# A fourth resident row group in a fused deformable-convolution kernel, with the second image's input kept between its passes and its table built backwards

## Chip, cores and metric

The kernel runs on one NeuronCore of a Trainium2 chip. The metric is the device time of one execution in microseconds (us). The kernel before took 3757.64 us, the median of three runs (3755.66 to 3757.74).

## What is computed

Input `x` is (2, 256, 128, 128) in fp32: two images, 256 channels, 128 by 128 pixels. Two layers follow each other, both of the form x + conv(group norm(x)). Cut to what matters:

```python
# layer 0: deformable 3x3 convolution on the normalised input
g = gn(x)                                    # 32 groups of 8 channels
offset = conv2d(g, w_off, b_off)             # 18 channels: dy, dx for each of 9 taps
mask = sigmoid(conv2d(g, w_mask, b_mask))    # 9 channels
# each tap of each pixel samples g at a fractional place: four corners, bilinear weights
sampled = bilinear(g, base + offset) * mask
x = x + einsum('bckhw,ock->bohw', sampled, w_conv) + b_conv
# layer 1: eight low-rank experts (a 1x3 into 8 channels, a 3x1 back to 256), mixed by probs
x = x + einsum('e,ebchw->bchw', probs, experts(gn(x)))
```

Group norm needs the mean and variance of a whole image before its first pixel can be normalised. So layer 0 needs statistics of `x`, and layer 1 statistics of layer 0's whole result.

## The kernel before, in words

**The table.** Sampling is done by gathers from a table in device memory, one per image. Each of its cells (a padded pixel) holds the 256 normalised channels of that pixel and those of the pixel below it: 512 floats, 2 KB. Two neighbouring cells, 4 KB, are the four corners of one sample. `frame` (L133) writes the zero cells around a table. To make the rest, `x` is normalised, TensorE transposes it from channels on partitions to pixels on partitions, ScalarE or VectorE copies the result out of PSUM into a tile of rows, and `store_cells` (L195) writes each row twice, as upper and as lower half of a cell.

**Sizes.** A group is 8 image rows (`GR`), a chunk 4 (`CR`): 16 groups (`NG`) or 32 chunks (`NCH`) an image. A tile of a group of `x` holds 1 MB (8 KB a partition), of a chunk half of that.

**The head** (L418 to L502) loads all of image 0, takes its statistics (L437), writes both frames (L453) and makes table 0. Of the loaded groups the first `XB + XR` = 6 stay on chip for the residual.

**The stream** (L814 to L842) is one loop over 2304 units, 1152 an image. A unit is one tap of one image row: 128 samples. In step s of it, `gather` (L546) issues the indirect DMA of unit s + 15 from GpSimd's queue (128 x 4 KB = 512 KB each, 15 tiles in turn), `product` (L556, ScalarE) multiplies the first corner of unit s + 3, `add` (L563, VectorE) adds the other three corners with three operations, `turn` (L570) transposes the sample on TensorE, `keep` (L580, ScalarE) copies it from PSUM, and `apply_tap` (L586, TensorE) multiplies with the convolution's weights. After the nine taps of a chunk `residual` (L596) adds `x` in place, `result_stats` (L602) takes the statistics for layer 1, and `store_x1` (L606) writes a finished group to the scratch tensor `x1`, unless `stays` (L283) says that the group remains on chip.

**Work between the units.** Everything else is a piece that `put` (L522) hangs on a slot, the number of the unit at whose step it is issued. The order of instructions on each engine, and of DMAs on SP's queue (SyncE's), is the order in which this loop meets them. Engines run in order, and so does SP: a DMA that must wait for a tile holds back the ones behind it. Pieces that matter here:
- `load_x` (L527) loads group g + 1 of the image at 54 slots before group g begins (L789), for the offsets (`offsets_of`, L298) and the residual.
- `table_beside(1)` (L610) makes image 1's table during image 0's units. From slot 4, every 8 slots, it loads a chunk into pool `tx` (three tiles) and takes its statistics (`of_stats`, L621, 14 and 18 slots later). After the norm's small pieces it loads all 32 chunks again from slot 324, one every 22 slots, normalises them in place (L631, 20 slots after the load), transposes and copies them (L635, L638) and writes their cells (L663, 33 slots after the load), going down the image. Row 0 of each tile of rows is copied from the tile before (L626).
- `second` (L803) runs layer 1 of image 0 during image 1's units, from the last chunk up, one chunk every 33 slots, with `cx`, `cxn` and `ch` pools of 4, 1 and 4 tiles (L804). Chunks whose group stayed on chip are used in place, the others are loaded from `x1` (L685).

**The tail** (L845 to L858) does layer 1 of image 1, by groups.

**Where groups of x live.** `x_tile` (L278) takes a tile of pool `xr` (`XR` = 3 tiles) for the last three groups of each image and for groups 3 to 5 of image 0, else one of pool `xp` (`XB` = 3 tiles) in turn. `stays` keeps the last three groups of image 0 and the last six of image 1.

Of the kernel before, what the change touches and what calls it, by code (L numbers as in the profile page):

```python
# [31 lines left out]
F32 = mybir.dt.float32  # L32
I32 = mybir.dt.int32
AF = mybir.ActivationFunctionType
# [4 lines left out]
P = 128  # L39
B, C, H, W = 2, 256, 128, 128  # L40
NH = C // P
# [6 lines left out]
CR = 4  # L48
NCH = H // CR
N = CR * W  # L50
GR = 8
CPG = GR // CR
NG = H // GR
GN = GR * W
WP = W + 3
HP = H + 3
CELL = 2 * C
# [4 lines left out]
UPG = UPC * CPG  # L62
UPI = UPG * NG
UNITS = B * UPI
GA = 15
# [1 line left out]
TL = 1  # L67
KL = 2
LM = 8
XB, XR = 3, 3  # L70


@with_exitstack
def layers(ctx, tc, x, w_om, b_om, w_cv, b_cv, w_in, w_out, probs, out):
    nc = tc.nc
# [5 lines left out]
    cp = ctx.enter_context(tc.tile_pool(name="const", bufs=1))  # L81
# [20 lines left out]
    )  # L102
    eps = cp.tile([P, 1], F32, name="eps")
    nc.vector.memset(eps, EPS)
    zero = cp.tile([P, CELL], F32, name="zero")
    nc.vector.memset(zero, 0.0)


# [14 lines left out]
    bias = cp.tile([P, NO], F32, name="bias")  # L123
# [9 lines left out]
    def frame(b):  # L133

        t = tables[b]
        side = t[WP - 1 : WP - 1 + (HP - 1) * WP].rearrange("(r c) e -> r c e", c=WP)[:, 0:3]
        z3 = zero.unsqueeze(1).broadcast_to([P, 3, CELL])
        nc.sync.dma_start(t[0:P], zero)
        nc.sync.dma_start(t[P : WP - 1], zero[0 : WP - 1 - P])
        nc.sync.dma_start(t[(HP - 1) * WP + 2 : (HP - 1) * WP + 2 + W], zero)  # L140
        nc.sync.dma_start(side[0:P], z3)
        nc.sync.dma_start(side[P : HP - 1], z3[0 : HP - 1 - P])
        nc.sync.dma_start(t[HP * WP - 1 : HP * WP + 2], zero[0:3])


    def norm_pieces(stats, small, psum, tag, name):
# [33 lines left out]
    def cells(b, y0, ny):  # L180
        rows = tables[b][(y0 + 2) * WP : (y0 + 2 + ny) * WP]
        return rows.rearrange("(r c) e -> c r e", c=WP)[2 : 2 + W]
# [5 lines left out]
    def transposes(ps, xt, rows):  # L188
        for i, r in enumerate(rows):
            for h in range(NH):  # L190
                nc.tensor.transpose(
                    ps[:, i, h * P : (h + 1) * P], xt[:, h, r * W : (r + 1) * W], ident
                )

    def store_cells(b, y, px, r, n):  # L195

        rows = px[:, r]
        pairs = bass.AP(rows.tensor, rows.offset, [rows.ap[0], [C, n], [1, CELL]])
        nc.sync.dma_start(cells(b, y + r, n), pairs)

    def store_last(b, row):

        nc.sync.dma_start(cells(b, H - 1, 1)[:, 0, 0:C], row)
        nc.sync.dma_start(cells(b, H - 1, 1)[:, 0, C:CELL], zero[:, :C])


    def offset_pieces(norm, oc, psum, tag, name):
# [62 lines left out]
    def pool(stack, name, bufs, **kw):  # L270
        return stack.enter_context(tc.tile_pool(name=name, bufs=bufs, reuse_waits="tile", **kw))

    xp = pool(ctx, "x", XB, side="right")
    xr = pool(ctx, "x_stay", XR, side="right")

    def x_tile(b, g):  # L278
        if g >= NG - XR or b == 0 and XB <= g < XB + XR:
            return xr.tile([P, NH, GN], F32, tag="xr", name=f"x_{b}_{g}")  # L280
        return xp.tile([P, NH, GN], F32, tag="xt", name=f"x_{b}_{g}")

    def stays(b, g):  # L283
        return g >= NG - XR - (XB if b == B - 1 else 0)
# [8 lines left out]
    xts = {}  # L293
# [124 lines left out]
    with ExitStack() as s:  # L418
# [6 lines left out]
        stats = hs.tile([P, NH, NCH, 6], F32, name="hstats")  # L425
        xv = view(x, 0)
        xs = []
        for g in range(NG):
            if g < XB + XR:
                xt = xts[0, g] = x_tile(0, g)  # L430
# [46 lines left out]
        head_norm(0)  # L477
        for g in range(NG):
            px = hp.tile([P, GR + 1, C], F32, tag="hp", name=f"hpx_{g}")
            nc.gpsimd.tensor_copy(px[:, 0], last[:, GR] if g else zero[:, :C])  # L480
            if g != 1 and g + 1 < NG:
                head_norm(g + 1)
            for i in range(0, GR, 2):
                ps = ht.tile([P, 2, C], F32, tag="t", name=f"hpt_{g}_{i}")
                transposes(ps, xs[g], (i, i + 1))
                if i % 4 == 0:
                    nc.scalar.copy(px[:, 1 + i : 3 + i], ps)
                else:
                    nc.vector.tensor_copy(px[:, 1 + i : 3 + i], ps)  # L489
                if g == 0:  # L490
                    store_cells(0, -1, px, i, 2)

                for piece in samples[: 2 if g < 2 else 1]:
                    piece()
                del samples[: 2 if g < 2 else 1]
            if g == 1:
                head_norm(2)
            if g > 0:
                store_cells(0, GR * g - 1, px, 0, GR)
            last = px  # L500
        store_last(0, last[:, GR])
        assert not samples  # L502


# [17 lines left out]
    def put(slot, piece, opens=False):  # L522
        sched[slot].append(piece)
        if opens:
            opened.add(slot)
# [82 lines left out]


    def table_beside(b):  # L610
        xq = pool(sides, "tx", 3)
        pq = pool(sides, "tpx", 2)
        held = {}
        xv = view(x, b)
        stats = st.tile([P, NH, NCH, 6], F32, tag="tstats", name=f"tstats_{b}")

        def load(j, what):
            held[what, j] = xq.tile([P, NH, N], F32, tag="tx", name=f"{what}_{b}_{j}")
            nc.sync.dma_start(held[what, j], xv[:, :, j * N : (j + 1) * N])

        def of_stats(j, h):  # L621
            nc.vector.bn_stats(stats[:, h, j], held["xs", j][:, h])

        def start(j):
            px = held["px", j] = pq.tile([P, CR + 1, C], F32, tag="tp", name=f"tpx_{b}_{j}")
            nc.vector.tensor_copy(px[:, 0], held["px", j - 1][:, CR] if j else zero[:, :C])  # L626

        def normalise(j, h):
            _, rstd, shift = norms0[b]
            v = held["xt", j][:, h]  # L630
            nc.scalar.activation(v, v, AF.Identity, bias=shift[:, h : h + 1], scale=rstd[:, h : h + 1])  # L631

        def turn_rows(j, i):
            ps = held["ps", j, i] = p_m.tile([P, 2, C], F32, tag="m", name=f"tpt_{b}_{j}_{i}")
            transposes(ps, held["xt", j], (i, i + 1))  # L635

        def keep_rows(j, i):
            nc.scalar.copy(held["px", j][:, 1 + i : 3 + i], held.pop(("ps", j, i)))  # L638

        slot = 4  # L640
        for j in range(NCH):
            put(slot, lambda j=j: load(j, "xs"))
            for h in range(NH):
                put(slot + 14 + 4 * h, lambda j=j, h=h: of_stats(j, h), True)
            slot += 8
        slot += 36
        norms0[b], pieces = norm_pieces(stats, st, p_m, "m", f"0_{b}")
        for piece in pieces:
            put(slot, piece)
            slot += 2  # L650
        offs[b], pieces = offset_pieces(norms0[b], oc, p_m, "m", str(b))
        for n, piece in enumerate(pieces):
            put(slot + 2 * n, piece)
        slot += 4
        for j in range(NCH):
            put(slot, lambda j=j: load(j, "xt"))
            for h in range(NH):
                put(slot + 20 + 3 * h, lambda j=j, h=h: normalise(j, h))
            put(slot + 24, lambda j=j: start(j))
            for n, i in enumerate(range(0, CR, 2)):  # L660
                put(slot + 26 + 4 * n, lambda j=j, i=i: turn_rows(j, i))
                put(slot + 28 + 4 * n, lambda j=j, i=i: keep_rows(j, i))
            put(slot + 33, lambda j=j: store_cells(b, CR * j - 1, held["px", j], 0, CR))  # L663
            slot += 22
        put(slot + 14, lambda: store_last(b, held["px", NCH - 1][:, CR]))
        return slot + 15


    def experts(b, norm, pools, psums, put_, rows, order, first, step, ahead, early=0):
# [107 lines left out]
    def expert_pools(stack, *bufs):  # L777
        return [pool(stack, name, n) for name, n in zip(("cx", "cxn", "ch"), bufs)]


    for b in range(B):
        stats1[b] = st.tile([P, NH, NCH, 6], F32, tag=f"stats{b}", name=f"stats1_{b}")
    for G in range(B * NG):
        b, g = divmod(G, NG)
        slot = UPG * G
        if g == 0:
            put(slot - 98, lambda b=b: load_x(b, 0))
        if g + 1 < NG:
            put(slot - 54, lambda b=b, g=g: load_x(b, g + 1))  # L789
        if (b, g) != (0, 0):  # L790
            for n, piece, opens in offsets_of(b, g):
                put(slot - 68 - GA + n, piece, opens)
    norms1 = [None] * B
    tabled = table_beside(1)
    assert tabled < UPI - UPG
    put(UPI - 16, sides.close)
    slot = UPI + LM + 10
    norms1[0], pieces = norm_pieces(stats1[0], st, p_m, "m", "1_0")
    for piece in pieces:
# [1 line left out]
        slot += 2  # L801

    def second(slot):  # L803
        pools = expert_pools(sides, 4, 1, 4)  # L804
        psums = ((p_m, "m"), (p_m, "m"))
        experts(0, norms1[0], pools, psums, put, CR, range(NCH - 1, -1, -1), slot + 36, 33, 33)

# [93 lines left out]
```

## Time and profile before

| what | value |
|---|---|
| median of three runs | 3757.64 us |
| profiled execution, its own time | 4080.06 us |
| its span (first to last instruction) | 4078.3 us |
| first gather issued | 155.7 us |
| last product of the stream | 3869.8 us |
| PE, PEld busy | 3493.9 us, 1854.9 us |
| VectorE (DVE), ScalarE (ACT), GpSimd (POOL) busy | 3355.3, 1841.9, 2290.3 us |
| bytes moved by DMA | 1444.29 MB, 354 GB/s over the span |
| of these by the gathers (queue q0) | 1208.11 MB |
| of these by SP's queue (q1) | 232.92 MB |

PE is TensorE's matmul, PEld its weight load. The page gives busy time by engine, a strip of 40 slices, the DMA queues, and groups of equal instructions with their mean time and with the idle time just before them, by what ended it. Times of single instructions come from one profiled execution, which is longer than the timed runs. VectorE's instructions overlap a little at their ends, so their mean time (481 ns for the adds of L566) is more than busy time by count (2963.7 us for 6912).

### The profile page before, as it was taken

The numbers are of one execution on the slowest core, as the hardware profiler recorded it, in microseconds if no ns is written. First come the engines' busy times: TensorE is split into PE (matmuls) and PEld (weight loads), VectorE is DVE, ScalarE is ACT, GpSimd is POOL, SyncE is SP. The second block draws the span as 40 slices with busy tenths as digits, with TensorE's granted clock in tenths as the row PEclk, the third lists the DMA queues.
The fourth block names the chain that finished last, engine by engine and source line by source line (L and its number), as shares of the span: only waits on it lengthen the run. The fifth ranks groups of instructions, "written<-read, shape, count | busy, mean of one in ns | idle before, by whom it ended". The sixth has DMA issues, their size and how long they took to land. (4 is left out here: it accounts for less than half of the span.)

```text
span 4078.3 us, 51366 instructions
## 1 busy us (share of the span) xinstructions
PE 3493.9 (86%) x13916; PEld 1854.9 (45%) x13916; DVE 3355.3 (82%) x7922; ACT 1841.9 (45%) x3883; POOL 2290.3 (56%) x2337
## 2 busy tenths in 40 slices
PE   3588888888888888988888999988999998888999
PEld 3444434444444444444444554444554555444433
DVE  6499988898888888988888888888898888888822
ACT  2344444455454554554444444444444444444421
POOL 0366655666666566666666665656666565656500
PEclk9699999999999999999999999999999999999999
DMA  9999999999999999999899999999999999999843
GB/s 366 368 377 379 380 356 354 375 385 388 375 402 396 374 404 394 387 398 367 325 336 349 359 371 347 365 365 348 364 361 370 356 361 356 351 335 344 304 150 124
DMA packets 427186, 1444.29 MB, mean 354 GB/s; under 512 B 42110, under 2 KB 43262, under 8 KB 426772
## 3 DMA queue, kind: packets, MB, share of 16 engines
q0 software_dynamic: 331776, 1208.11, 78.3%
q1 hardware_dynamic: 95124, 232.92, 15.1%
q8 instruction: 113, 1.85, 0.2%
q14 instruction: 173, 1.42, 0.1%
HBM read 1312.88 MB, written 127.97 MB: 353 GB/s over the span
## 5 line engine op out<-in xcount | busy, mean ns | idle before, releaser
L566 DVE SCALAR_TENSOR_TENSOR acc<-g,wt,acc 128x256 f32<-128x256 f32 x6912 | 2963.7, 481 | 417.0 <-ACT acc L560 250.3
L550 POOL DMA_INDIRECT g<-table,cidx x2304 | 2279.5, 989 | 1438.9 <-DVE acc L566 523.1
L591 PE MATMUL po<-sm,wcv 128*128 128x512 f32 x4608 | 2483.9, 621 | 278.8 <-issue 129.9
L584 ACT COPY sm<-ptr 128x512 f32<-128x512 f32 x1152 | 671.7, 583 | 1797.3 <-PE ptr L576 1035.4
L576 PEld LDWEIGHTS ptr<-idp,acc 128*128 128x128 f32 x4608 | 626.6, 145 | 1567.8 <-issue 1070.4
L560 ACT ACTIVATE acc<-g,wt 128x256 f32<-128x256 f32 x2304 | 1063.2, 506 | 81.5 <-DMA g<-table,cidx 59.0
L576 PE MATMUL ptr<-idp,acc 128*128 128x128 f32 x4608 | 929.2, 284 | 158.9 <-DVE acc L566 56.6
L591 PEld LDWEIGHTS po<-sm,wcv 128*128 128x128 f32 x4608 | 746.2, 197 | 343.8 <-issue 167.3
L319 PE MATMUL pu<-wus,x 128*128 128x81 f32 (+2 forms) x1600 | 297.2, 313 | 4.9 <-issue 3.3
L319 PEld LDWEIGHTS pu<-wus,x 128*128 128x128 f32 x1600 | 239.4, 200 | 8.0 <-issue 4.3
L707 PE MATMUL ph<-xcn,win 128*64 128x254 f32 (+3 forms) x1152 | 191.4, 474 | 16.0 <-issue 12.5
L600 DVE SCALAR_TENSOR_TENSOR x<-po,bcv,x 128x512 f32<-128x512 f32 x128 | 95.4, 745 | 64.5 <-remote 39.2
L745 DVE TENSOR_TENSOR xc<-pe,xc 128x512 f32<-128x512 f32 x92 | 60.3, 684 | 98.1 <-issue 79.1
L707 PEld LDWEIGHTS ph<-xcn,win 128*64 128x64 f32 x1152 | 84.1, 144 | 102.2 <-issue 76.2
L721 PE MATMUL pe<-h,wout 128*128 128x256 f32 (+1 forms) x384 | 126.4, 457 | 1.8 <-DVE xc L745 1.1
L714 ACT ACTIVATE h<-ph,pr 128x256 f32<-128x256 f32 (+1 forms) x48 | 26.2, 547 | 173.3 <-PE ph L707 139.1
L604 DVE BATCH_NORM_STATS2 stats<-x 128x6 f32<-128x512 f32 x128 | 87.7, 685 | 0.1
L721 PEld LDWEIGHTS pe<-h,wout 128*128 128x128 f32 x384 | 67.2, 191 | 41.1 <-issue 37.6
L745 DVE TENSOR_TENSOR x<-pe,x 128x512 f32<-128x512 f32 x36 | 23.1, 684 | 65.9 <-PE pe L736 62.3
L736 PE MATMUL pe<-h,wout 64*128 64x128 f32 (+1 forms) x752 | 69.9, 321 | 0.8 <-issue 0.8
L334 PE MATMUL om<-u,idp 128*128 128x216 f32 x192 | 53.1, 358 | 20.1 <-ACT u L328 11.7
L489 DVE COPY hpx<-hpt 128x512 f32<-128x512 f32 x32 | 21.1, 687 | 55.2 <-DMA table<-hpx 45.3
(92 smaller groups left out, 779.5 us busy)
## 6 DMA issues: line engine op xcount, KB each, us to landing
g<-table,cidx POOLq DMA_INDIRECT x2304
x<-in_x_dram SPq DMA_DIRECT2D x32, 1024.0 KB
table<-tpx SPq DMA_DIRECT2D x32, 1024.0 KB
table<-hpx SPq DMA_DIRECT2D x15, 2048.0 KB
x<-x SPq DMA_DIRECT2D x23, 1024.0 KB
out_dram<-xc SPq DMA_DIRECT2D x46, 512.0 KB
xs<-in_x_dram SPq DMA_DIRECT2D x32, 512.0 KB
xt<-in_x_dram SPq DMA_DIRECT2D x32, 512.0 KB
```

The lines of the kernel that those rows point to most:

```text
L319: nc.tensor.matmul(held["ps", j][:, lo:hi], lhsT=xt[:, h, r * W : (r + 1) * W], rhs=w[:, lo - i + 2 : hi - i + 2], start=(i == 2 and h == ...
L550: nc.gpsimd.indirect_dma_start(out=gt[:], out_offset=None, in_=tables[b][:, :], in_offset=bass.IndirectOffsetOnAxis(ap=idx[:, rr, k : k + ...
L560: nc.scalar.activation(acc, gts[u][:, 0:C], AF.Copy, scale=wt[:, 0, rr, k : k + 1])
L566: nc.vector.scalar_tensor_tensor(accs[u], gt[:, q * C : (q + 1) * C], wt[:, q, rr, k : k + 1], accs[u], ALU.mult, ALU.add)
L576: nc.tensor.transpose(pts[u // 2][:, h, (r % 2) * W : (r % 2 + 1) * W], acc[:, h * P : (h + 1) * P], ident)
L584: nc.scalar.copy(sms[u // CR][:, :, (r - 1) * W : (r + 1) * W], pts.pop(u // 2))
L591: nc.tensor.matmul(pos_[b, ci, m], lhsT=wcv[:, h, k, m * P : (m + 1) * P], rhs=sms[u // CR][:, h], start=(k == 0 and h == 0), stop=(k == K ...
L600: nc.vector.scalar_tensor_tensor(v, pos_.pop((b, ci, m)), bcv[:, m : m + 1], v, ALU.add, ALU.add)
L604: nc.vector.bn_stats(stats1[b][:, m, ci], xts[b, ci // CPG][:, m, at_ : at_ + N])
L707: nc.tensor.matmul(o[:, :, to], lhsT=win[:, h, tap], rhs=pairs[:, t, :, of], start=(q == 0), stop=(q == 5),)
L721: nc.tensor.matmul(ps[t][:, m], lhsT=wout[:, 2 * t, m * P : (m + 1) * P], rhs=hs[ci], start=(banks or m == 0), stop=False,)
L745: nc.vector.tensor_tensor(v, ps[t][:, ms].rearrange("p h (j x) -> p h j x", x=W), v, ALU.add)
```

## The change

`XR` goes from 3 to 4, and the tiles for it are found by making others fewer: `zero` is half as wide, pool `tx` has two tiles instead of three, the expert pools 3, 1 and 3, and the statistics of image 1's table share a tile with those of its result.

With it, four groups of image 0 and seven of image 1 stay on chip for layer 1, and groups 0 to 6 of image 0 stay from the head. `xp` becomes three tiles of one buffer each, named by g modulo 3 (for image 1 by -g modulo 3).

In `table_beside(1)` the last four groups of image 1 are loaded by groups into the `xr` tiles for the statistics (the first groups of image 0 have left these by then), stay there, and are normalised in place for the table. The table is made from the last chunk up, so that these tiles are free for image 0's last groups. The first three groups are loaded by groups into `xp` tiles, normalised into a `tx` tile, and stay for image 1's offsets and residual. The row that two tiles of rows share is copied the other way, and the first row's cells are written last (`store_top`). Chunks are 10 slots apart in the statistics and 21 in the table. The writes of `frame` take `zero` in pieces of 256 floats.

```diff
 LM = 8
-XB, XR = 3, 3
+XB, XR = 3, 4
...
     nc.vector.memset(eps, EPS)
-    zero = cp.tile([P, CELL], F32, name="zero")
+    zero = cp.tile([P, C], F32, name="zero")
     nc.vector.memset(zero, 0.0)
...
         side = t[WP - 1 : WP - 1 + (HP - 1) * WP].rearrange("(r c) e -> r c e", c=WP)[:, 0:3]
-        z3 = zero.unsqueeze(1).broadcast_to([P, 3, CELL])
-        nc.sync.dma_start(t[0:P], zero)
-        nc.sync.dma_start(t[P : WP - 1], zero[0 : WP - 1 - P])
-        nc.sync.dma_start(t[(HP - 1) * WP + 2 : (HP - 1) * WP + 2 + W], zero)
-        nc.sync.dma_start(side[0:P], z3)
-        nc.sync.dma_start(side[P : HP - 1], z3[0 : HP - 1 - P])
-        nc.sync.dma_start(t[HP * WP - 1 : HP * WP + 2], zero[0:3])
+        side = side.rearrange("r c (a e) -> r (c a) e", a=2)
+        for to in (
+            t[0:P], t[P : WP - 1], t[(HP - 1) * WP + 2 : (HP - 1) * WP + 2 + W],
+            t[HP * WP - 1 : HP * WP + 2],
+        ):
+            to = to.rearrange("r (a e) -> r a e", a=2)
+            n = to.shape[0]
+            nc.sync.dma_start(to, zero[0:n].unsqueeze(1).broadcast_to([n, 2, C]))
+        for to in (side[0:P], side[P : HP - 1]):
+            n = to.shape[0]
+            nc.sync.dma_start(to, zero[0:n].unsqueeze(1).broadcast_to([n, 6, C]))
...
         nc.sync.dma_start(cells(b, y + r, n), pairs)
-    def store_last(b, row):
-        nc.sync.dma_start(cells(b, H - 1, 1)[:, 0, 0:C], row)
-        nc.sync.dma_start(cells(b, H - 1, 1)[:, 0, C:CELL], zero[:, :C])
...
-    xp = pool(ctx, "x", XB, side="right")
+    xp = pool(ctx, "x", 1, side="right")
     xr = pool(ctx, "x_stay", XR, side="right")
-    def x_tile(b, g):
-        if g >= NG - XR or b == 0 and XB <= g < XB + XR:
-            return xr.tile([P, NH, GN], F32, tag="xr", name=f"x_{b}_{g}")
-        return xp.tile([P, NH, GN], F32, tag="xt", name=f"x_{b}_{g}")
+    def x_tile(b, g, what="x"):
+        if g >= NG - XR or b == 0 and g < XR:
+            return xr.tile([P, NH, GN], F32, tag="xr", name=f"{what}_{b}_{g}")
+        n = (-g if b else g) % XB
+        return xp.tile([P, NH, GN], F32, tag=f"xt{n}", name=f"{what}_{b}_{g}")
...
             px = hp.tile([P, GR + 1, C], F32, tag="hp", name=f"hpx_{g}")
-            nc.gpsimd.tensor_copy(px[:, 0], last[:, GR] if g else zero[:, :C])
+            nc.gpsimd.tensor_copy(px[:, 0], last[:, GR] if g else zero)
             if g != 1 and g + 1 < NG:
...
             last = px
-        store_last(0, last[:, GR])
+        nc.sync.dma_start(cells(0, H - 1, 1)[:, 0, 0:C], last[:, GR])
+        nc.sync.dma_start(cells(0, H - 1, 1)[:, 0, C:CELL], zero)
         assert not samples
...
     def table_beside(b):
-        xq = pool(sides, "tx", 3)
+        xq = pool(sides, "tx", 2)
         pq = pool(sides, "tpx", 2)
...
         xv = view(x, b)
-        stats = st.tile([P, NH, NCH, 6], F32, tag="tstats", name=f"tstats_{b}")
+        stats = st.tile([P, NH, NCH, 6], F32, tag=f"stats{b}", name=f"tstats_{b}")
...
+        def load_group(g, what):
+            xt = held[what, "g", g] = x_tile(b, g, what)
+            nc.sync.dma_start(xt, xv[:, :, g * GN : (g + 1) * GN])
+            if g < XB:
+                xts[b, g] = xt
+        def place(j, what):
+            g, i = divmod(j, CPG)
+            if (what, "g", g) in held:
+                return held[what, "g", g][:, :, i * N : (i + 1) * N]
+            return held[what, j]
         def of_stats(j, h):
-            nc.vector.bn_stats(stats[:, h, j], held["xs", j][:, h])
+            nc.vector.bn_stats(stats[:, h, j], place(j, "xs")[:, h])
         def start(j):
             px = held["px", j] = pq.tile([P, CR + 1, C], F32, tag="tp", name=f"tpx_{b}_{j}")
-            nc.vector.tensor_copy(px[:, 0], held["px", j - 1][:, CR] if j else zero[:, :C])
+            nc.vector.tensor_copy(px[:, CR], held["px", j + 1][:, 0] if j + 1 < NCH else zero)
         def normalise(j, h):
             _, rstd, shift = norms0[b]
-            v = held["xt", j][:, h]
-            nc.scalar.activation(v, v, AF.Identity, bias=shift[:, h : h + 1], scale=rstd[:, h : h + 1])
+            g = j // CPG
+            v = place(j, "xs" if g >= NG - XR else "xt")
+            if h == 0:
+                held["xn", j] = v
+                if g < XB:
+                    held["xn", j] = xq.tile([P, NH, N], F32, tag="tx", name=f"xn_{b}_{j}")
+            nc.scalar.activation(
+                held["xn", j][:, h], v[:, h], AF.Identity, bias=shift[:, h : h + 1],
+                scale=rstd[:, h : h + 1],
+            )
...
             ps = held["ps", j, i] = p_m.tile([P, 2, C], F32, tag="m", name=f"tpt_{b}_{j}_{i}")
-            transposes(ps, held["xt", j], (i, i + 1))
+            transposes(ps, held["xn", j], (i, i + 1))
         def keep_rows(j, i):
-            nc.scalar.copy(held["px", j][:, 1 + i : 3 + i], held.pop(("ps", j, i)))
+            nc.scalar.copy(held["px", j][:, i : i + 2], held.pop(("ps", j, i)))
+        def store_top():
+            nc.sync.dma_start(cells(b, -1, 1)[:, 0, 0:C], zero)
+            nc.sync.dma_start(cells(b, -1, 1)[:, 0, C:CELL], held["px", 0][:, 0])
...
         for j in range(NCH):
-            put(slot, lambda j=j: load(j, "xs"))
+            g, i = divmod(j, CPG)
+            if g < NG - XR:
+                put(slot, lambda j=j: load(j, "xs"))
+            elif i == 0:
+                slot = max(slot, UPG * (g - NG + XR + 1) + LM + 12)
+                put(slot, lambda g=g: load_group(g, "xs"))
             for h in range(NH):
                 put(slot + 14 + 4 * h, lambda j=j, h=h: of_stats(j, h), True)
-            slot += 8
-        slot += 36
+            slot += 10
+        slot += 18
         norms0[b], pieces = norm_pieces(stats, st, p_m, "m", f"0_{b}")
...
             put(slot + 2 * n, piece)
-        slot += 4
-        for j in range(NCH):
-            put(slot, lambda j=j: load(j, "xt"))
+        slot -= 12
+        for j in range(NCH - 1, -1, -1):
+            g, i = divmod(j, CPG)
+            if g < XB and i == CPG - 1:
+                put(slot, lambda g=g: load_group(g, "xt"))
+            elif XB <= g < NG - XR:
+                put(slot, lambda j=j: load(j, "xt"))
             for h in range(NH):
...
                 put(slot + 28 + 4 * n, lambda j=j, i=i: keep_rows(j, i))
-            put(slot + 33, lambda j=j: store_cells(b, CR * j - 1, held["px", j], 0, CR))
-            slot += 22
-        put(slot + 14, lambda: store_last(b, held["px", NCH - 1][:, CR]))
-        return slot + 15
+            put(slot + 33, lambda j=j: store_cells(b, CR * j, held["px", j], 0, CR))
+            slot += 21
+        put(slot + 13, store_top)
+        return slot + 14
...
-    for b in range(B):
+    def result_stats_of(b):
         stats1[b] = st.tile([P, NH, NCH, 6], F32, tag=f"stats{b}", name=f"stats1_{b}")
+    result_stats_of(0)
     for G in range(B * NG):
...
     tabled = table_beside(1)
-    assert tabled < UPI - UPG
+    assert tabled < UPI - GA - 16
     put(UPI - 16, sides.close)
+    put(UPI, lambda: result_stats_of(1))
     slot = UPI + LM + 10
...
     def second(slot):
-        pools = expert_pools(sides, 4, 1, 4)
+        pools = expert_pools(sides, 3, 1, 3)
         psums = ((p_m, "m"), (p_m, "m"))
```

## The prediction

> **What bounds the kernel now.** I read the page's busy table first, then the stretches of the stream one by one, then the waits inside them. The profiled execution took 4080.06 us, a span of 4078.3 with 1.8 around it. From the page:
>
> ```profile
> DVE  6499988898888888988888888888898888888822
> DMA  9999999999999999999899999999999999999843
> q0 software_dynamic: 331776, 1208.11, 78.3%
> q1 hardware_dynamic: 95124, 232.92, 15.1%
> ```
>
> VectorE is at eight or nine tenths and the DMA engines at nine nearly everywhere, so the two compete for the bound. Five sixths of the bytes are the gathers of q0, which the change leaves alone; it can only touch q1. The next view cuts the span where the plan changes: head, statistics of image 1, its table, rest of image 0, image 1, tail. I found the cuts by counting the products of L560, one per unit (324, 707 and 124 in the three stages of image 0, 1152 in image 1). The columns are window, length, busy us of PE, PEld, DVE, ACT, POOL, then PE clock, DMA share, GB/s:
>
> ```profile
> 0.00:162.00 162.00, 65.30 (x348) 58.51 (x348) 82.33 (x149) 39.79 (x55) 15.69 (x38) 0.84 0.99 365
> 162.00:681.00 519.00, 431.41 (x1539) 216.73 (x1540) 471.04 (x1113) 227.06 (x498) 323.54 (x327) 0.93 0.98 372
> 681.00:1814.00 1133.00, 969.89 (x3655) 515.65 (x3653) 974.19 (x2350) 573.73 (x1217) 703.95 (x708) 0.94 1.00 387
> 1814.00:2016.00 202.00, 168.21 (x602) 85.74 (x600) 171.17 (x412) 87.70 (x194) 125.09 (x127) 0.94 0.95 359
> 2016.00:3878.00 1862.00, 1673.68 (x6982) 903.12 (x6981) 1609.65 (x3821) 864.05 (x1874) 1122.06 (x1138) 0.96 0.94 351
> 3878.00:4079.00 201.00, 185.42 (x797) 75.15 (x795) 46.88 (x79) 49.56 (x52) 0.00 (x0) 0.97 0.37 139
> ```
>
> VectorE is densest in the statistics stage (471 of 519). The table stage has the highest rate and a share of 1.00. A full share alone doesn't prove a DMA bound. That does:
>
> ```profile
> 1482.00:1508.00 26.00, 23.89 (x97) 13.11 (x96) 23.88 (x57) 14.58 (x31) 16.98 (x17) 1.00 1.03 410
> 1590.00:1618.00 28.00, 27.57 (x113) 14.69 (x112) 27.23 (x65) 16.41 (x33) 17.27 (x19) 1.00 1.03 410
> ```
>
> ```profile
> 1491.89 0.51 ACT L560 ACTIVATE acc<-g,wt 128x256 f32<-128x256 f32 x1 [1.46 <-DMA g<-table,cidx]
> 1493.84 0.51 ACT L560 ACTIVATE acc<-g,wt 128x256 f32<-128x256 f32 x1 [0.97 <-DMA g<-table,cidx]
> ```
>
> In these windows, inside the table stage, the products wait for gathers one after another, and the rate is 410 GB/s both times. I take 410 as what the DMA engines give this mix. Elsewhere gathers aren't late:
>
> ```profile
> ACT acc L560 <- DMA g<-table,cidx: 59.0, 54, 18.7
> ACT sm L584 <- PE ptr L576: 1035.4, 592, 8.6
> DVE acc L566 <- ACT acc L560: 250.3, 80, 9.2
> ```
>
> Only 59.0 us of ScalarE's waits are for gathers. Many of VectorE's stalls come behind a ScalarE copy that waits for TensorE's transposes, in stops of up to 8.6 us.
>
> **From the profile to the timed runs.** The timed median, 3757.64, is 322 us below the profiled execution. In the stream (162 to 3878) VectorE worked 471.0 + 974.2 + 171.2 + 1609.7 = 3226 of 3716 us and idled 490; I assume that the 322 lies in that idle time. A floor by stage then says who binds, with bytes at 0.410 MB/us:
> - Statistics: 471 by VectorE; bytes 320 gathers x 0.524 + 16.8 statistics + 5.2 other = 189.8 MB, or 463. VectorE, narrowly.
> - Table (units 324 to 1030): 974 by VectorE. Bytes: 706 gathers 370.2, table reads 16.8, table writes 33.6, nine x loads and nine x1 stores 18.9, in all 439.4 MB, or 1072. DMA, by 98.
> - Rest: 171 by VectorE, about 166 by bytes. Image 1: 1610 by VectorE; 351 GB/s x 1862 us = 654 MB, or 1594. VectorE, narrowly.
>
> With head and tail: 162 + 471 + 1072 + 171 + 1610 + 201 = 3687, so some 69 us of stalls are left in a timed run. That the floor comes under the median but close supports it.
>
> [...] beside q1's table traffic the gathers are late, and almost only there. [...] I use 410. [...] in the trace's packet records a 2048-byte packet of SP's queue takes 88 ns, a 1024-byte one 67, not half.
>
> **The change part by part.** Instruction counts on PE, ACT and POOL stay; VectorE does the same sums. What changes is SP's list, 12.58 MB fewer:
> - Chunks 24 to 31 aren't read again for the table: 4.19 MB, all in the table stage. At 0.410 that is 10.2 us.
> - The x1 store of image 0's group 12 goes (unit 947): 1.05 MB, table stage, 2.6 us. Table stage together 12.8. The table now starts at unit 358 with chunks 21 apart, not 324 and 22, so the light part comes first: (1.049/21) + (2.097/72) + 0.524 = 0.603 MB a unit, 1.47 us, still over VectorE's 974/707 = 1.38; then 0.628 MB, 1.53 us. Both parts stay DMA bound, so the bytes count nearly whole, and what is late next is still the gather: VectorE comes 98 - 12 = 86 us later. I take 12.
> - Group 6 isn't loaded twice (unit 306, 1.05 MB); image 1's groups 0 to 2 aren't either (3.15 MB around the images' border); one x1 store and two half-group loads fewer in image 1 (2.10 MB). VectorE binds there: 0 each; if that cover is gone, 6.3 / 0.41 = 15.4. The last megabyte is in the tail, where PE is busy 185 of 201: 0.
> - The statistics loads come 10 units apart, not 8, still 64 BN stats of 684 ns: 0, or a gain of a few us where that stage is near both bounds.
> - The frame's 1302 zero pieces of 2 KB become 2604 of 1 KB, ahead of the head's table writes on SP's queue. Cost (2604 x 67 - 1302 x 88)/16 = 3.7 us of every engine. By the fastest and slowest 1 KB packets of the trace (46, 77 ns) 0.3 to 5.4. The engines have short gaps there, the writes behind are DMA bound: +2.5.
> - New waits: the load of group 15's statistics goes out 9 units after the x1 store whose tile it takes; the next on SP's queue is 63 units later. The expert's load now waits for the store of three chunks before, not four, and is still needed 33 units later, about 48 us. I price both at 0; the bound is the fourth rival.
>
> Sum: -12 + 2.5 = -9.5, so 3757.6 - 9.5 = 3748. In a profiled execution it will look smaller: its table stage took 1133, over the DMA floor.
>
> **The rivals.**
> 1. The forecast, table stage DMA bound and the rest not: 3740 to 3755: 0.45.
> 2. VectorE and the PE stalls hide the traffic; only the frame shows. For: 59 us of waits on gathers in all, 18.7 of it the very first. Against: the 410 windows, and that the timed runs are faster, thus hungrier. 3757.6 + 2.5 = 3760: 0.23.
> 3. DMA binds more deeply than the floor says, in the statistics stage and image 1 also (463 against 471, 1594 against 1610: a ceiling 2% lower is enough). Then the stream's 11.5 MB count whole: 28.1 - 2.5 = 25.6, 3732: 0.17.
> 4. Slower: the statistics' reads lose their spare tile (pool tx two, not three). A load can go out only when the chunk two before is read, and is read itself some 16 units later, about 23 us. If it lands later, BN stats waits, and with it VectorE, which binds that stage. For:
>
> ```profile
> SPq L619 <- DVE tstats L622: 157.5, 10, 52.0
> ```
>
> SP already waits for free tiles. Against: BN stats of L622 idled 0.0 us before. It decides from a landing time of 23 us; 24 loads late by 1 us each are 24, so 3748 + 24 = 3772: 0.15.
>
> That the change doesn't do what it says is excluded: SP's list does have the loads fewer.
>
> **How the numbers follow.** A measurement of this kernel tells about 0.2%, 7.5 us, from no change: 3750.1 and 3765.2 are the borders. Faster: 0.17 of rival 3 and 0.34 of the forecast's 0.45, 0.51. Within: 0.11 of the forecast, 0.20 of rival 2, 0.31. Slower: 0.18 (rival 4 and 0.03 of rival 2). The range takes in most of rival 3 and rival 2 and the frame's worst: 3728 to 3765. The forecast's own range is 3740 to 3755.
>
> **What would show it.** Right: table reads down by eight, SP's bytes near 220 MB, the table stage's floor lower, waits of L560 on gathers fewer in it, the head 2 to 4 us longer. Wrong: BN stats of the statistics idling (rival 4), or the median unmoved with fewer bytes (rival 2); a gain beyond 20 us would mean a lower ceiling in the timed runs than 410.

## The result, and the profile after

The changed kernel took 3741.36 us (median of 6 runs, 3739.01 to 3743.70), the kernel before 3756.11 (6 runs, 3755.66 to 3757.74). The ratio is 0.9960, with a 95% interval of 0.9949 to 0.9971: faster by 14.75 us, where 9.5 was forecast. The time lies inside the range and inside the forecast's own range.

The profiled execution of after took 3743.08 us, and its page answers the first lines shown of before:

```profile
DVE  6499999999888889899999999999999999999812
DMA  9999999999999999999999999999999999999743
q0 software_dynamic: 331776, 1208.11, 82.0%
q1 hardware_dynamic: 89898, 220.33, 15.4%
```

The gathers of q0 are the same 1208.11 MB; SP's queue moved 12.59 MB less, as counted. The strip of DVE is denser than in the first profile of before, which was 322 us longer than the timed runs and can't be compared with this one stage by stage. The first experiment therefore profiled before once more.

### The profile page after: what moved, and what is told of

Read it like the earlier page. It is cut to its first block, busy times and chain, and to the rows that moved or that the text cites. A ratio compares the mean times of both kernels' runs of the same rounds, so it can differ in the third digit from the quotient of the medians.

```text
span 3741.3 us, 51320 instructions
## 1 busy us (share of the span) xinstructions
PE 3379.1 (90%) x13916; PEld 1799.5 (48%) x13916; DVE 3354.6 (90%) x7922; ACT 1918.1 (51%) x3883; POOL 2381.9 (64%) x2337
## 3 DMA queue, kind: packets, MB, share of 16 engines
q0 software_dynamic: 331776, 1208.11, 82.0%
q1 hardware_dynamic: 89898, 220.33, 15.4%
## 5 line engine op out<-in xcount | busy, mean ns | idle before, releaser
L554 POOL DMA_INDIRECT g<-table,cidx x2304 | 2371.0, 1029 | 1007.6 <-DVE acc L570 391.9
L595 PE MATMUL po<-sm,wcv 128*128 128x512 f32 x4608 | 2404.5, 604 | 162.6 <-ACT sm L588 84.0
L564 ACT ACTIVATE acc<-g,wt 128x256 f32<-128x256 f32 x2304 | 1120.3, 507 | 806.4 <-DMA g<-table,cidx 656.2
L580 PEld LDWEIGHTS ptr<-idp,acc 128*128 128x128 f32 x4608 | 607.2, 142 | 1459.7 <-issue 726.1
L588 ACT COPY sm<-ptr 128x512 f32<-128x512 f32 x1152 | 664.8, 577 | 728.7 <-PE ptr L580 727.0
L580 PE MATMUL ptr<-idp,acc 128*128 128x128 f32 x4608 | 909.1, 279 | 92.9 <-DVE acc L570 71.7
L595 PEld LDWEIGHTS po<-sm,wcv 128*128 128x128 f32 x4608 | 725.5, 192 | 221.8 <-ACT sm L588 112.4
L321 PE MATMUL pu<-wus,x 128*128 128x81 f32 (+2 forms) x1448 | 261.0, 306 | 0.0
L321 PEld LDWEIGHTS pu<-wus,x 128*128 128x128 f32 x1448 | 208.5, 193 | 1.9
L748 PE MATMUL ph<-xcn,win 128*64 128x254 f32 (+3 forms) x1152 | 177.8, 458 | 3.1 <-ACT xcn L731 3.1
L777 PEld LDWEIGHTS pe<-h,wout 64*128 64x128 f32 x752 | 51.8, 187 | 25.6 <-issue 16.9
## 6 DMA issues: line engine op xcount, KB each, us to landing
x<-in_x_dram SPq DMA_DIRECT2D x29, 1024.0 KB, 12.6
```

What stands on the lines that cost most here:

```text
L321: nc.tensor.matmul(held["ps", j][:, lo:hi], lhsT=xt[:, h, r * W : (r + 1) * W], rhs=w[:, lo - i + 2 : hi - i + 2], start=(i == 2 and h == ...
L554: nc.gpsimd.indirect_dma_start(out=gt[:], out_offset=None, in_=tables[b][:, :], in_offset=bass.IndirectOffsetOnAxis(ap=idx[:, rr, k : k + ...
L564: nc.scalar.activation(acc, gts[u][:, 0:C], AF.Copy, scale=wt[:, 0, rr, k : k + 1])
L580: nc.tensor.transpose(pts[u // 2][:, h, (r % 2) * W : (r % 2 + 1) * W], acc[:, h * P : (h + 1) * P], ident)
L588: nc.scalar.copy(sms[u // CR][:, :, (r - 1) * W : (r + 1) * W], pts.pop(u // 2))
L595: nc.tensor.matmul(pos_[b, ci, m], lhsT=wcv[:, h, k, m * P : (m + 1) * P], rhs=sms[u // CR][:, h], start=(k == 0 and h == 0), stop=(k == K ...
```

## The experiments

A time "over after" is measured against 3741.36. After was not timed again beside these edits at this pace; before was, and its median lay between 3757.04 and 3757.37 there, against 3756.11 in the result. So a time over after is uncertain by about 1 us. Ratios are to before, run on the same chip in alternation.

### Before, profiled again (e0)

No edit.

> The kernel before, unchanged, for a second profile: the first one took 4080 us and had stops of several us that the changed kernel's profile (3743) does not have. Theory (table stage DMA bound): a span near 3754, the table stage (units 324 to 1030) near 1085 to 1100 us at about 405 GB/s, waits of L560 on gathers several hundred us. Rival 'VectorE hides the traffic': waits on gathers stay under 100 us. Rival 'DMA binds in the other stages too': waits on gathers in image 1 as dense as in the table stage.

It took 3758.54 us, span 3756.8. The windows by stage, first of this profile of before, then of after (columns as in the prediction; the cuts lie at the same counts of products, within two):

```profile
161.00:641.00 480.00, 416.21 (x1538) 204.91 (x1539) 470.30 (x1112) 243.80 (x499) 334.20 (x327) 0.99 1.02 402
641.00:1726.00 1085.00, 953.18 (x3668) 509.62 (x3667) 987.11 (x2361) 599.03 (x1216) 743.76 (x708) 0.97 1.02 404
1726.00:1899.00 173.00, 155.15 (x571) 78.69 (x570) 162.73 (x392) 93.56 (x193) 124.23 (x122) 0.97 1.01 392
1899.00:3547.00 1648.00, 1596.22 (x6970) 873.82 (x6969) 1600.70 (x3814) 903.98 (x1871) 1172.33 (x1146) 1.00 1.01 399
3547.00:3757.00 210.00, 194.90 (x828) 80.35 (x828) 54.73 (x98) 51.56 (x56) 0.00 (x0) 0.97 0.35 133
```

```profile
162.00:641.00 479.00, 417.89 (x1532) 204.87 (x1532) 465.40 (x1098) 243.13 (x498) 336.38 (x328) 0.98 1.02 400
641.00:1718.00 1077.00, 948.68 (x3674) 503.83 (x3672) 988.54 (x2372) 598.90 (x1215) 738.39 (x707) 0.98 1.02 402
1718.00:1886.00 168.00, 153.98 (x571) 75.83 (x570) 163.10 (x395) 94.37 (x193) 125.34 (x123) 0.99 1.01 394
1886.00:3531.00 1645.00, 1594.97 (x6970) 873.68 (x6968) 1600.06 (x3813) 889.97 (x1869) 1166.08 (x1145) 1.00 1.01 398
3531.00:3742.00 211.00, 195.33 (x829) 80.43 (x828) 55.28 (x99) 52.12 (x57) 0.00 (x0) 0.97 0.34 127
```

The stages of before (480, 1085, 173, 1648) stand close to the prediction's floors (471, 1072, 171, 1610). VectorE's idle time in these four stages is 3386 - 3220.8 = 165 us, against 490 in the first profile: the 322 us did lie there. After gains 8 us in the table stage, 5 in the rest of image 0, 3 in image 1 and 1 in the statistics, and loses 1 in the head and 1 in the tail: 15 in all. Taken between the starts of the same products, the table stage repeats within 1 us in profiles that share its plan (1077.8, 1077.2 and 1077.5 in after, e3 and e6b; 1085.3 and 1084.5 in e0 and e1). Image 1 repeats less well: 1642.6 to 1646.1 us in six profiles with after's image 1, 1648.3 and 1647.3 in the two with before's, so its 3 may be 1 to 6. The rate near 400 GB/s in every stage of the stream is the first sign that the DMA engines matter outside the table stage too. The waits say it outright, in the whole span of this profile of before:

```profile
ACT acc L560 <- DMA g<-table,cidx: 854.2, 1115, 18.2
ACT sm L584 <- PE ptr L576: 523.3, 438, 3.9
```

Waits on gathers are 854.2 us here, against 59.0 in the first profile. By stage they are 177 us in the statistics, 374 in the table stage, 58 in the rest of image 0 and 247 in image 1: about a third of the time all through image 0, and 15% in image 1. So gathers are late well outside the table stage, though in image 1 not as densely as in the table stage, which the last rival needed. After has 656.2:

```profile
ACT sm L588 <- PE ptr L580: 727.0, 582, 4.0
ACT acc L564 <- DMA g<-table,cidx: 656.2, 863, 17.4
```

The 198 us by which the waits shrank are no gain of that size: the span is 15 us shorter. ScalarE is busy for 51% of the span in both, and what it no longer waits for gathers it waits for TensorE's transposes (523.3 to 727.0). Such a wait shows what is late, not what it costs.

### The frame alone (e1)

Before, with only the frame's zeros in 1 KB pieces:

```diff
-        z3 = zero.unsqueeze(1).broadcast_to([P, 3, CELL])
-        nc.sync.dma_start(t[0:P], zero)
...
+        side = side.rearrange("r c (a e) -> r (c a) e", a=2)
...
+            nc.sync.dma_start(to, zero[0:n, :C].unsqueeze(1).broadcast_to([n, 2, C]))
```

> Before, with the frame's zero cells written in pieces of 1 KB instead of 2 KB and nothing else. Theory: the head 2.5 us longer (0.3 to 5.4), so 3758.6. Rival 'the frame lies beside the norm's arithmetic': 3756.1, no change.

3759.09 us against 3757.37 (ratio 1.0004, interval 0.9996 to 1.0013): 1.7 us more, not told apart from nothing. The first product moves as little: it comes at 161.2 us in e0, 163.7 in e1, 162.0 in after.

### The table's last groups read again (e2)

After, but chunks 24 to 31 are read a second time at their places in the table, into the tiles that hold them (the same data, 4.19 MB):

```diff
+        def again(j):
+            nc.sync.dma_start(place(j, "xs"), xv[:, :, j * N : (j + 1) * N])
...
+            elif g >= NG - XR:
+                put(slot, lambda j=j: again(j))
```

> After, but the chunks 24 to 31 are read again into their tiles before they are normalised for the table: 4.19 MB back on SP's queue in the table stage, the output unchanged. Theory: 4.19 / 0.41 = 10.2 us more than after's 3741.4, so 3751.6. Rival 'VectorE hides the traffic' (the gain then came from the other spacing of the statistics and the table): 3741 to 3743.

3747.47 us (3746.01 to 3749.67), ratio 0.9975 (0.9965 to 0.9984): 6 us over after, not 10.2. The trace shows where it is paid. Units 324 to 420 of the table stage, then 420 to 526, first in after, then in e2:

```profile
641.00:782.00 141.00, 127.79 (x492) 65.24 (x490) 138.41 (x346) 75.02 (x159) 97.02 (x98) 0.99 1.00 385
782.00:940.00 158.00, 143.70 (x572) 76.27 (x572) 151.44 (x362) 90.45 (x185) 110.86 (x106) 1.00 1.02 406
```

```profile
641.00:782.00 141.00, 126.31 (x492) 64.27 (x490) 138.40 (x347) 75.24 (x160) 96.72 (x98) 1.00 1.01 392
782.00:947.00 165.00, 143.97 (x570) 76.48 (x569) 152.65 (x361) 90.96 (x185) 110.96 (x106) 1.00 1.03 410
```

The first rows hold the same units, and so do the second ones. SP sent four of the eight reads in each (at units 344, 382, 396 and 416, then at 438, 457, 479 and 500; from the third on, each 0.4 us behind the table store that stands before it in the queue).

In the first window VectorE is busy 138.4 of 141 us, and ScalarE waits for gathers 0.0 us in after and 0.4 in e2. The rate is under 410, and e2 moves about 1.0 MB more (392 GB/s against 385) in the same time. In the second window the rate stands at its 410, e2 moves about 3.5 MB more, and the same work takes 7 us longer.

What lies between is a stock. The landings in e2's trace show on average three gathers landed ahead of the one in use in units 324 to 391, one in units 391 to 420, and none in units 460 to 1030, where each product takes its gather as it lands (in after's trace 3.2, 2.8 and 0.0 on average). The program has 15 tiles for gathers (`GA = 15`), but never more than five have landed ahead in the stream of e2, nor more than six in that of after. While the rate has room or the stock lasts, a byte costs nothing here (1.0 MB more in the same 141 us); after that it is paid for (3.5 MB more, 7 us). After's own gain in the table stage lies in the same place: before takes 164 us for units 420 to 526 where after takes 157, and both take 778 to 779 for the 504 units behind.

### The first groups of image 1 loaded again (e3)

After, but groups 0 to 2 of image 1 are loaded again where before loaded them, into the tiles that hold them (3.15 MB):

```diff
-        if (b, g) not in xts:
-            xts[b, g] = x_tile(b, g)
+        if (b, g) not in xts or b == 1 and g < XB:
+            if (b, g) not in xts:
+                xts[b, g] = x_tile(b, g)
```

> After, but image 1's groups 0 to 2 are read again into their tiles at the slots where before reads them (units 1054 to 1170): 3.15 MB back around the border of the images. Theory (VectorE binds there): 3741 to 3743. Rival 'DMA binds in the other stages too': 3.15 / 0.41 = 7.7 us more, 3749.

3748.23 us (3745.47 to 3749.19), ratio 0.9974 (0.9964 to 0.9984): 5 to 7 us over after, by the ratios or by the times, of the 7.7 that the bytes would be worth in full. The expected 0 was wrong. The cost lies right behind the table stage, in units 1030 to 1060. First e0, then after, then e3:

```profile
1726.00:1776.00 50.00, 40.33 (x146) 21.29 (x145) 42.44 (x102) 24.70 (x52) 30.58 (x30) 0.93 1.03 410
```

```profile
1718.00:1761.00 43.00, 39.03 (x149) 20.84 (x148) 40.84 (x99) 25.00 (x51) 30.78 (x30) 0.96 1.03 412
```

```profile
1718.00:1769.00 51.00, 42.71 (x156) 22.47 (x154) 43.66 (x106) 25.06 (x52) 30.52 (x30) 0.93 1.03 412
```

The rate is 410 to 412 GB/s in all three. VectorE is busy 41 to 44 us each time, so it doesn't bind where 50 pass. SP sends e3's three loads right behind the table's last store, at unit 1047. The table stage hands over with the gathers behind, and loads that come before they have caught up are paid for.

A rival for e2 and e3 would be that an engine waits for the added loads themselves. The traces exclude it: from 200 to 3540 us, in e2, e3, e6b and e7 alike, no engine but SP waits for any DMA other than a gather. The added bytes cost time by making gathers late: in e2 from 782 to 945 us the waits on DMAs are ScalarE's 48.3 us and GpSimd's 4.3, all for gathers.

### Chunks of the table 23 apart (e4b)

```diff
-            slot += 21
+            slot += 23
```

> The same kernel as in the run before with the table 23 slots apart. In that run TensorE stopped for microseconds again and again and every kernel, before and after too, took about 4190 us; there nothing that changes traffic told, as a theory of spare DMA time would have it. At the pace of the 3757 us runs the expectation stands: 4 to 7 us less than after, 3735 to 3738, a ratio to before of 0.9945; rival 0.996, as after.

3735.00 us (3733.57 to 3739.04), ratio 0.9945 (0.9931 to 0.9958): 6.4 us under after, as expected, and the fastest of all. Its table stage and rest of image 0, cut at the counts of products of after's windows of 1077 and 168 us:

```profile
641.00:1709.00 1068.00, 947.49 (x3650) 500.57 (x3649) 989.04 (x2373) 593.50 (x1206) 739.97 (x707) 0.98 1.02 402
1709.00:1881.00 172.00, 155.56 (x594) 80.17 (x593) 163.03 (x394) 99.26 (x203) 124.96 (x122) 0.99 1.02 401
```

No byte was taken away. The same table traffic is spread over 64 more units: the table stage takes 9 us less, and the rest of image 0, where 3 to 4 MB went by these rates (the expectation had 6), 4 us more. So the premise that the gathers are ahead there holds only in part, as e3 shows too, and about half of the gain is paid back. That is what a DMA bound stage with VectorE not far behind would do. The wider spacing also spreads the table's work on the other engines. That was not tried apart, but the rate is 402 GB/s in both table stages, which speaks for the bytes.

### Chunks of the statistics 8 apart (e5b)

Rival to all of the above: the gain is in the wider spacing of the statistics, not in the bytes.

```diff
-            slot += 10
+            slot += 8
```

> The statistics 8 slots apart, once more, at the pace of the 3757 us runs: 3740 to 3744, a ratio to before of 0.9955 to 0.9965; rival 'the wider spacing is where after's gain comes from': 0.998 or more.

3738.42 us, ratio 0.9952 (0.9938 to 0.9965): a little under the 3740 to 3744 expected, and not slower than after, so the wider spacing gives nothing. Whether 8 is a little better stays open, the intervals overlap.

### Image 1's loads twice (e6b)

After, but groups 3 to 11 of image 1 are read twice for layer 1 (9.44 MB more):

```diff
+            for _ in range(2 if b == 1 and g < NG - XR else 1):
+                nc.sync.dma_start(xts[b, g], view(x, b)[:, :, g * GN : (g + 1) * GN])
```

> Image 1's groups 3 to 11 read twice, once more, at the pace of the 3757 us runs: 0 to 6 us more than after, a ratio to before of 0.996 to 0.9975; rival 'DMA binds image 1 too': 23 us more, 1.002.

3757.31 us, ratio 1.0003 (0.9994 to 1.0011): 16 us over after, where the bytes are worth 9.44 / 0.41 = 23 in full. The expectation of a few us fell. Image 1's window in e6b took 1662 us against 1645 in after, and its waits on gathers are 321.8 us, against 143.0 in after and 246.7 in e0. First e6b, then after:

```profile
ACT acc L565 <- DMA g<-table,cidx: 321.8, 461, 2.5
```

```profile
ACT acc L564 <- DMA g<-table,cidx: 143.0, 207, 2.2
```

About two thirds of the price of an added megabyte show. Half of the 16 us comes from units 1500 to 1700. First after, then e6b:

```profile
2381.00:2672.00 291.00, 282.85 (x1271) 160.78 (x1272) 281.25 (x665) 159.59 (x328) 204.36 (x199) 1.00 1.02 405
```

```profile
2386.00:2685.00 299.00, 284.77 (x1264) 160.41 (x1263) 279.30 (x659) 160.21 (x326) 206.41 (x199) 0.99 1.02 405
```

The rate stays at 405 GB/s when three groups (3.15 MB) are added, and the time grows by 8 us, their full price. So the bytes already count there in after, with 66.7 us of waits on gathers, though VectorE is busy 281 of 291 us. At the ends of image 1 (units 1152 to 1300 and 2100 to 2304) after's rate is only 389 and 390, and VectorE binds: it is busy 203.7 of 208 and 279.3 of 285 us, and ScalarE's waits on gathers are 0.0 and 4.5. The floors of the prediction were means over the whole stage and hid this.

### The same bytes, earlier (e7)

If e2's cost is one of place, the same 4.19 MB must cost less ahead of the table. After, with the last four groups read a second time at units 276 to 340:

```diff
+        def again(g):
+            nc.sync.dma_start(held["xs", "g", g], xv[:, :, g * GN : (g + 1) * GN])
...
+                put(slot + 32, lambda g=g: again(g))
```

> After, with the last four groups of image 1 read a second time 32 slots after their first read (units 276 to 340) instead of from unit 358 on: the same 4.19 MB as in the run that reads them again for the table, but where after's gathers are ahead and its rate is 366 to 391 GB/s. The room there up to unit 420 is (410 - 391) x 93 us + (410 - 366) x 51 us + (410 - 395) x 90 us, some 5 MB. Theory (bytes cost time only once the gathers are behind): 0 to 3 us more than after, a ratio to before of 0.996 to 0.9968. Rival 'bytes cost the same wherever they stand': as the reads for the table or the full 10.2 us, 0.9975 to 0.9987.

3743.83 us (3741.67 to 3744.35), ratio 0.9964 (0.9951 to 0.9978): 2.5 us over after, and every run of it below every run of e2. The time is lost and mostly regained, in the stretch of the reads (units 260 to 324) and in the one behind it. First after, then e7:

```profile
548.00:641.00 93.00, 82.20 (x303) 39.14 (x301) 91.54 (x218) 46.52 (x100) 64.51 (x65) 1.00 1.01 391
```

```profile
545.00:645.00 100.00, 85.69 (x314) 41.53 (x313) 96.63 (x230) 48.39 (x99) 67.37 (x66) 0.99 1.02 408
645.00:782.00 137.00, 123.86 (x484) 64.31 (x483) 134.24 (x336) 79.00 (x160) 100.18 (x96) 1.00 1.02 398
```

7 us longer while the reads last, at 408 GB/s; then units 324 to 420 take 137 us where after takes 141, and both kernels start unit 420 at 782 us. A late gather is caught up where the plan is lighter. The 2 us that are left are lost in units 420 to 526 (159 against 157 us).

### Where the bytes don't count (a0, e4, e5, e6)

On one chip all kernels took about 4190 us, before too (4191.49), and after gave 4192.75 (ratio 0.9993, interval 0.9976 to 1.0010). Three of the edits above ran in it first.

> After, unchanged, on the same chip as the next three, as their reference: 3741.4, ratio to before 0.996.

> After, with the table's chunks 23 slots apart instead of 21, so that the table ends near unit 1108 instead of 1044. The bytes stay, some 6 MB of them move from the table stage into units 1030 to 1152, where after's rate is 393 GB/s and the gathers are ahead. Theory (what counts is bytes while the gathers are behind): 4 to 7 us less than after, 3735 to 3738. Rival 'the bytes cost the same wherever they stand in image 0': 3741.

> After, with the chunks of the statistics 8 slots apart, as in before, instead of 10; the rest of the plan follows some 50 slots earlier. It undoes one part. Theory (DMA and VectorE both near their bounds in the first 80 units, where before's profile is 3 us longer): 1 to 3 us more than after, less what an earlier table gains at its end: 3740 to 3744. Rival 'the wider spacing is where after's gain comes from': 3749 or more.

> After, with image 1's groups 3 to 11 each read twice in a row into their tile: 9.44 MB more, spread over image 1's units, output unchanged. Theory (VectorE binds image 1, with 1600 us of work there against 642 + 9.4 MB in 1589 us at 410 GB/s): 0 to 6 us more than after, 3741 to 3747. Rival 'DMA binds image 1 too': 9.44 / 0.41 = 23 us more, 3764.

Nothing came out as expected: 4188.57 (e4, interval 0.9977 to 1.0006), 4192.43 (e5, 0.9981 to 1.0015) and 4187.47 (e6, 0.9979 to 1.0002), so neither 12.6 MB fewer nor 9.4 MB more shows. The waits of after there, and its group of products, tell why:

```profile
ACT sm L588 <- PE ptr L580: 1061.3, 568, 10.2
```

```profile
L564 ACT ACTIVATE acc<-g,wt 128x256 f32<-128x256 f32 x2304 | 1064.3, 506 | 59.7 <-DMA g<-table,cidx 44.6 <-issue 9.6 <-DVE acc L570 4.8
```

ScalarE waits for TensorE's transposes, up to 10.2 us at a time, and for gathers only 44.6 us in all: the picture of the first profile of before (1035.4 and 59.0). TensorE's mean granted clock was 0.939 here and 0.946 there, against 0.98 in the runs of 3735 to 3760. Another 565.5 us of the same copies' waits are ended by what the profile only calls "remote" (450.9 in the first profile of before); e0, after and e6b have no such wait. By these waits the stops set the pace there, and gathers are hardly ever late. What the stops come from was not found.

## Why the prediction was right, and where it was off

**The bound.** Taking the 322 us as idle time that the timed runs don't have was right (165 us of idle against 490), and so was reading the DMA bound from two windows at 410 GB/s instead of from the sum of waits. Rival 2, which rested on the 59 us, falls: in e0 they are 854.2. What else the prediction took from the first profile falls with it: "Elsewhere gathers aren't late" and "almost only there" hold for that profile alone. In e0 the gathers are late in the statistics too (177 of 480 us), and the traces with every landing (e1, e2, e4b, e6b) show hardly a gather ahead of its product in units 0 to 260 (on average 0.01 in after's).

**Table stage: 12 predicted, 8 measured.** The mechanism holds (e2, e4b); the term "both parts stay DMA bound, so the bytes count nearly whole" was too large. It compared averages, 1.47 us a unit by bytes with 1.38 by VectorE. In units 324 to 420 VectorE's work is more, 138.4 / 96 = 1.44 us a unit, and the bytes are fewer, 385 GB/s x 141 us = 54.3 MB, or 1.38 us a unit at 410 GB/s: the first store of the table goes out only at unit 395. So VectorE binds there, the DMA engines have room, and a few gathers lie in stock. E2 puts the eight chunks at 6 us, not 10.2. The removed x1 store (2.6 priced) was not tried alone; the 504 units that it stands in take as long as before, but the later plan also moves table traffic into them, so its worth stays open.

**Elsewhere: 0 predicted, about 9 measured.** This was the step that failed: "VectorE binds there: 0 each; if that cover is gone, 6.3 / 0.41 = 15.4". In the border of the images the gathers are still behind from the table stage (e3: 5 to 7 us of 7.7 come back). In image 1 the floors of 1610 and 1594 were told apart as if 16 us in 1600 were a margin, and as if the bytes lay evenly; e6b shows about 0.7 of the full price per byte, which for the 2.10 MB saved there is 0.7 x 5.1 = 3.6, and 3 were seen (1 to 6 by the scatter of that stage). Rival 3 was half right: its places bind, but not whole. Its 28.1 us for the stream's bytes compare with 17 seen there.

**The frame: 2.5 predicted,** 1.7 measured, within the spread.

**The waits: 0 predicted, and so it is.** Rival 4 needed the statistics to wait for their reads. In after they don't: their idle time is 0.0, so whatever SP waits before it can send the loads of L623, the statistics' among them, costs nothing. From the groups of after, then from its SP waits:

```profile
L638 DVE BATCH_NORM_STATS2 tstats<-xs 128x6 f32<-128x512 f32 x64 | 44.0, 687 | 0.0
```

```profile
SPq L726 <- DMA out_dram<-xc: 160.4, 21, 8.7
SPq L623 <- DVE acc L570: 311.5, 20, 37.3
SPq L623 <- DVE tstats L638: 15.5, 2, 14.1
```

Reads landed in 8.3 us (median), far from the 23 at which the rival decides. The first of the SP lines is the expert's load that now waits for a store: 21 times, up to 8.7 us, with 48 us in hand; no wait of an engine on that load is in the trace.

In sum: 8 + 9 - 2 = 15, where 12 + 0 - 2.5 = 9.5 was forecast. Two errors of opposite sign made the total look better than its parts, and that it came to lie inside the forecast's own range is partly luck.

## What to carry to other kernels

Price a saved transfer by its place: nearly whole where the consumer waits for its transfers or has not yet caught up with them (e3: 5 to 7 us of 7.7), nothing where another engine binds and the DMA rate has room or landed buffers lie in stock (the first window of e2: 0 us for 1.0 MB at 392 GB/s, with VectorE busy 138.4 of 141 us), a part of it over a stage that has both (e6b: 16 us of 23). A floor by stage and resource is worth making, but a difference of 1% between two floors is a tie, not a cover, and a mean over a stage hides the stretch where the other resource binds. Before a sum rests on a profile, ask whether it is the regime of the timed runs: a profile 9% longer showed the waits of another bound (59.0 us for gathers, where e0 shows 854.2).

## What the runs showed of the hardware

The DMA engines held 392 to 404 GB/s in the four stages of the stream in e0 and after, 3.4 ms of gathers, loads and stores mixed, and 405 to 412 in the windows where added bytes cost time (e2, e3, e6b, e7). A DMA share of 1.00 came with less, too: 385 GB/s in after's window of 641 to 782 us, where ScalarE's waits on gathers are 0.0 us.

The same kernel took 3757 us on two chips and 4191 on a third, where ScalarE waited for TensorE's transposes up to 10.2 us at a time. In that regime a change in traffic of 9 to 13 MB could not be seen (4187.47 and 4192.75 us against 4191.49). Whether the chip or the moment makes it is open.
